# Sharing the PSUM copies of a projected product between two engines, in a triangle-multiplication and spectral kernel

## The chip, the cores and the metric

The kernel runs on one core of one Trainium2 chip. The metric is the device time of the whole program in microseconds, as the median of repeated runs. The core's engines have queues of their own, each worked off in order: PE (TensorE: matmuls and transposes, with PEld for the loading of weights), DVE (VectorE), ACT (ScalarE), POOL (GpSimd) and SP (SyncE, which issues most DMAs here). They meet at semaphores. PE writes into PSUM, and DVE and ACT read from there.

## What is computed

The input x has 512 x 512 positions with 64 channels. Layer 0 normalises it, gates two projections with a mask, multiplies them as a matrix product per channel, normalises that over the channels, projects it, gates it again and adds it to x. Layer 1 takes 12 x 12 Fourier modes of the result, mixes the channels and adds the inverse transform. The part that matters here is the normalisation of the product over the channels and its projection (the two lines that begin with `out = _ln` and `out = out @ out_w`).

```
x = x + _L0_conv_ref(_gn(x), ...)          # layer 0
    xn = _ln(x, norm_w, norm_b)
    left  = (xn @ left_w  + left_b)  * mask * sigmoid(xn @ lgate_w + lgate_b)
    right = (xn @ right_w + right_b) * mask * sigmoid(xn @ rgate_w + rgate_b)
    out_gate = sigmoid(xn @ ogate_w + ogate_b)
    out = einsum('bkjd,bkid->bijd', left, right)
    out = _ln(out, onorm_w, onorm_b)
    out = out @ out_w + out_b
    return out * out_gate
x = x + _L1_conv_ref(_gn(x), ...)          # layer 1: fft2, 12 x 12 modes, channel mixing, ifft2
```

## The kernel before

Rows whose mask is zero add nothing to the product, so the kernel gathers those whose mask is not zero into at most 256 ranks, and works on a product of 256 x 256 positions (`places`, in SBUF). The stages that lead there end at about 659 us of the span. Then one long loop (L1137) does two things in one sequence of steps s: first the *projected stage*, 64 groups that normalise and project the product, and then 256 groups that gate the result, add it to x and gather statistics (the gating loop, to about 1490 us). The last stage, to 1815 us, adds the inverse transform and stores the output.

A group is 8 x 64 = 512 elements per partition, and eight groups make a block (SIZE = 8); in step s = 8 k + n, n counts inside the block. The order of the instructions is the one written down (the schedule is manual). A step takes a group g through these stations, some steps apart:

- `transpose(s + 13)` (L979): PE transposes the group in four matmuls into `t_ps` (two buffers), and ACT copies it into `xt_y` (L988; two buffers).
- `centered(s + 12)` (L998): eight matmuls of 64 x 128 with the weights `both`. They write `y_ps`: in each half, 64 columns of the centred product and 64 of the projected one. It has two buffers, so that product g + 2 may start only when all readers of product g are done.
- `squared(s + 12)` (L1014): ACT squares the centred columns into `sq_c` (L1023) and then copies the projected columns into the group's slot of `xt_c` (L1024), a ring of 15 buffers.
- `summed(s + 11)` (L1026), in every other step: DVE sums the squares of two groups into `scratch`, a tile in PSUM.
- `root(k + 1)` (L1032), at n = 5: ACT takes the square root of a block's sums, once the sum of its last group (g % 8 = 7) is there. The first root loads ACT's table of functions.
- The reciprocal at n = 7 (L1204), on DVE.
- The multiplication `z_t` (L1211), DVE: the projected product, copied 12 steps earlier, times the reciprocal root. POOL adds the bias for two groups at a time (L1215), and SP stores the result in DRAM (`u_d`, L1220).

In the first 12 steps (the lead, LEAD = 13) there is no multiplication yet. POOL also issues the first gathers of x for the gating loop (L637) in this stage. When the last product is done, `y_ps` is closed and its PSUM goes to the matmuls of the gating loop (`c_ps`, `w_ps`; L1148).

Of the kernel before, what the change touches and what calls it, by code (L numbers as in the profile page):

```python
# [19 lines left out]
C = 64  # L20
# [26 lines left out]
def conv_preact_kernel(ctx: ExitStack, tc: tile.TileContext, t: dict):  # L47
    nc = tc.nc
# [572 lines left out]
    def compact(fc):  # L621
# [31 lines left out]
        with tc.tile_pool(name="xc", bufs=1) as cp:  # L653
# [56 lines left out]
            with tc.tile_pool(name="fb", bufs=QB + 8) as gp, tc.tile_pool(name="fw", bufs=2) as wk, tc.tile_pool(  # L710
# [18 lines left out]
                def centered(q):  # L729
                    cps = pc.tile([P, 8, C], F32, name="cc_ps")  # L730
                    for i in range(4):
                        nc.tensor.matmul(
                            cps[:, 2 * i : 2 * i + 2, :], gts[q][:, i * P : (i + 1) * P], center, start=True, stop=True
                        )
                    sq = wk.tile([P, 8, C], F32, name="sqc")
                    nc.scalar.activation(sq, cps, AF.Square)
                    k, n = divmod(q, QB)
                    if n == 0:
                        totals[k] = rp.tile([P, QB * 8], F32, name="total")
                    return sq, totals[k][:, 8 * n : 8 * n + 8]  # L740
# [82 lines left out]
        with tc.tile_pool(name="tri", bufs=1) as trp:  # L823
# [17 lines left out]
            with tc.tile_pool(name="ti", bufs=4) as ip, tc.tile_pool(name="tt", bufs=3) as tp, tc.tile_pool(  # L841
                name="tpt", bufs=4, space=PSUM
            ) as ps_t, tc.tile_pool(name="tpo", bufs=3, space=PSUM) as ps_o:
                for c in range(C):
                    sides = []
                    for name, src in (("left", left_d), ("right", right_d)):
                        raw = ip.tile([P, 2, K], F32, name=name + "_raw")
# [26 lines left out]
            SIZE = 8  # L874
            LEAD = 13
# [5 lines left out]
            with tc.manual_schedule(), tc.tile_pool(name="late", bufs=1) as lp:  # L881
# [65 lines left out]
                with tc.tile_pool(name="np_x", bufs=LEAD + 2) as tp, tc.tile_pool(  # L947
# [63 lines left out]
                    def raw(s):  # L1011
                        return xts[s].rearrange("p i (h c) -> p (i h) c", h=2)

                    def squared(s, cps):  # L1014
                        n = s % SIZE
                        if n % 2 == 0:
                            sqs[s // 2] = sqp.tile([P, 16, C], F32, name="sq_c")
                        sq = sqs[s // 2][:, 8 * (n % 2) : 8 * (n % 2) + 8, :]
                        if s >= first * SIZE:
                            nc.scalar.activation(sq, cps, AF.Square)  # L1020
                        else:
                            by_half = lambda t: t.rearrange("p (i h) c -> p h i c", h=2)
                            nc.scalar.activation(by_half(sq), cps[:, :, :, :C], AF.Square)  # L1023
                            nc.scalar.copy(by_half(raw(s)), cps[:, :, :, C:])  # L1024

                    def summed(s):  # L1026
                        k, n = divmod(s, SIZE)
# [109 lines left out]
                    for s in range(-LEAD, total_g + 2 * SIZE):  # L1137
# [16 lines left out]
                        if 0 <= s + LEAD - 1 < total_g:  # L1154
                            cps = centered(s + LEAD - 1)
# [9 lines left out]
                        if cps is not None:  # L1165
                            squared(s + LEAD - 1, cps)
# [304 lines left out]
```

## Time and profile before

| | |
|---|---|
| Median of three runs | 1818.94 us (1818.11 to 1819.47) |
| The profiled execution | 1816.82 us, its span 1815.0 us |
| Busy in the span | PE 1641.3 (90%), DVE 1424.5 (78%), ACT 961.3 (53%), POOL 945.1 (52%) |
| Projected stage, 659 to 768 us | PE 107.8, DVE 76.2, ACT 101.4, POOL 61.3 us busy of 109.0 |
| Change of stage, 768 to 800 us | PE 30.8, DVE 26.5, ACT 26.6, POOL 25.6 of 32.0 |
| Gating loop, 800 to 1490 us | PE 657.1, DVE 662.5, ACT 500.9, POOL 650.5 of 690.0 |
| Last stage, 1490 to 1815 us | PE 246.6, DVE 181.4, ACT 24.8, POOL 60.7 of 325.0; DMA engines busy throughout, 418 GB/s |
| Copies of the projected product (L1024) | 64 on ACT, 0.58 us each |

The profile is that of one execution, so its own time stands beside its span; the median of the runs is another figure. Shares of busy time over the span mix stages with different limits, and a stage is read by itself. Two instructions of one engine may overlap by about 0.1 us in the records, so that the distance from start to start says more about an engine's pace than the duration of one. The ends of matmuls are modelled, their starts are recorded.

### The profile page before, as it was taken

How to read it: one execution, taken by the hardware profiler on the slowest of the kernel's cores; microseconds unless marked ns; L12 is line 12 of the kernel's file. 1: busy time of each engine (PE TensorE's matmuls, PEld its weight loads, DVE VectorE, ACT ScalarE, POOL GpSimd, SP SyncE). 2: the span in 40 equal slices, each digit the busy share in tenths (PEclk: the TensorE clock that was granted, in tenths of full speed). 3: DMA queues.
4: the chain of work that ended last, by engine and by line, in shares of the span. 5: the costliest groups of instructions: out<-in, count | busy, mean ns of one | idle time of the engine just before them, and what ended most of it. 6: DMA issues, size and time to landing. Idle time of an engine off the chain costs nothing. (4 is left out here: it accounts for less than half of the span.)

```text
span 1815.0 us, 33640 instructions
## 1 busy us (share of the span) xinstructions
PE 1641.3 (90%) x11424; PEld 1287.8 (71%) x11424; DVE 1424.5 (78%) x2980; ACT 961.3 (53%) x1708; POOL 945.1 (52%) x711
## 2 busy tenths in 40 slices
PE   6779899999899999998999999999999977998772
PEld 6667666664688778897888888888888844665331
DVE  7989777777455547779999999999999996765442
ACT  3666555554222259986777777777777741011000
POOL 4665111111000006788999999999999892211120
PEclk9989999999899999999999999999999986555555
DMA  7999155556655513577777776777677689999999
GB/s 286 386 386 380 72 138 137 140 140 153 203 176 184 175 47 133 213 256 254 259 239 242 265 246 234 256 267 260 238 259 271 220 261 418 425 427 426 427 426 385
DMA packets 189525, 467.94 MB, mean 258 GB/s; under 512 B 34848, under 2 KB 134176, under 8 KB 148384
## 3 DMA queue, kind: packets, MB, share of 16 engines
q1 hardware_dynamic: 158160, 262.09, 42.5%
q0 software_dynamic: 27712, 201.40, 29.0%
q10 hardware_dynamic: 3472, 2.20, 0.5%
q8 instruction: 93, 1.52, 0.3%
q14 instruction: 88, 0.72, 0.1%
HBM read 278.05 MB, written 187.56 MB: 257 GB/s over the span
## 5 line engine op out<-in xcount | busy, mean ns | idle before, releaser
L995 PE MATMUL w_ps<-gate_x,xt_c 128*128 128x128 f32 x2048 | 281.1, 281 | 28.9 <-DVE z_t L1211 27.3
L1058 POOL TENSOR_TENSOR places<-places,z_t 128x1024 f32<-128x1024 f32 x127 | 301.0, 2370 | 8.1
L995 PEld LDWEIGHTS w_ps<-gate_x,xt_c 128*128 128x128 f32 x2048 | 252.6, 194 | 45.1 <-DVE z_t L1211 43.6
L995 PE MATMUL c_ps<-center_x,xt_c 128*128 128x128 f32 x2048 | 277.6, 279 | 1.2 <-ACT xt_c L1024 0.6
L995 PEld LDWEIGHTS c_ps<-center_x,xt_c 128*128 128x128 f32 x2048 | 253.6, 195 | 3.9 <-ACT xt_c L990 2.8
L1377 PE MATMUL l_ps<-places,rinv 24*128 24x512 f32 x512 | 207.4, 1127 | 30.1 <-DVE places L1384 18.8
L1113 DVE BATCH_NORM_STATS2 stats2c<-places 128x6 f32<-128x128 f32 x1024 | 220.4, 278 | 8.4 <-POOL places L1058 8.4
L1028 DVE TENSOR_REDUCE scratch<-sq_c 128x16 f32<-128x1024 f32 x160 | 194.5, 1216 | 27.9 <-ACT sq_c L1023 19.4
L1215 POOL TENSOR_TENSOR z_t<-z_t,bias_row_out 128x1024 f32<-128x1024 f32 x32 | 75.6, 2364 | 247.8 <-DVE z_t L1211 243.7
L1162 ACT ACTIVATE z_t<-z_t 128x1024 f32<-128x1024 f32 x128 | 135.5, 1058 | 130.6 <-DVE z_t L1217 129.1
L985 PE MATMUL t_ps<-c_ident,places 128*128 128x128 f32 x1280 | 199.6, 279 | 1.3 <-DVE places L870 1.3
L1377 PEld LDWEIGHTS l_ps<-places,rinv 24*128 24x128 f32 x512 | 120.3, 304 | 112.3 <-DVE places L1384 57.0
L985 PEld LDWEIGHTS t_ps<-c_ident,places 128*128 128x128 f32 x1280 | 145.1, 142 | 60.6 <-issue 52.9
L990 ACT ACTIVATE xt_c<-t_ps,ab_xc 128x512 f32<-128x512 f32 x256 | 176.0, 687 | 13.2 <-PE t_ps L985 12.1
L1211 DVE TENSOR_TENSOR z_t<-w_ps,rs_n 128x512 f32<-128x512 f32 x256 | 171.9, 672 | 8.3 <-PE w_ps L995 8.2
L1020 ACT ACTIVATE sq_c<-c_ps 128x512 f32<-128x512 f32 x256 | 150.5, 588 | 32.5 <-PE c_ps L995 32.0
L1217 DVE TENSOR_TENSOR z_t<-z_t,scratch 128x1024 f32<-128x1024 f32 x128 | 156.3, 1221 | 9.9 <-ACT rs_n L1034 3.7
L687 DVE BATCH_NORM_STATS2 stats1c<-x_ps 128x6 f32<-128x512 f32 x256 | 156.6, 682 | 8.0 <-PE x_ps L686 7.6
L1054 POOL TENSOR_TENSOR z_t<-z_t,places 128x1024 f32<-128x1024 f32 x64 | 151.5, 2368 | 13.9 <-ACT z_t L1162 13.8
L1384 DVE TENSOR_TENSOR places<-places,l_ps 128x512 f32<-128x512 f32 x176 | 109.2, 682 | 55.8 <-DMA places<-x_h,dst_i 43.9
L1054 POOL TENSOR_TENSOR z_t<-z_t,bias_row_out 128x1024 f32<-128x1024 f32 x63 | 149.3, 2370 | 5.7 <-ACT z_t L1162 5.4
L749 POOL COPY rbc<-rq_out 128x512 f32<-128x512 f32 x64 | 38.3, 613 | 210.2 <-DVE rq_out L214 132.0
(213 smaller groups left out, 2746.9 us busy)
## 6 DMA issues: line engine op xcount, KB each, us to landing
x_h<-places SPq DMA_DIRECT2D x64, 1024.0 KB
out_x<-places SPq DMA_DIRECT2D x44, 1024.0 KB
places<-u_d SPq DMA_DIRECT2D x512, 64.0 KB
out_x<-lx_t SPq DMA_DIRECT2D x20, 1024.0 KB
left_d<-o_c SPq DMA_DIRECT2D x64, 256.0 KB
right_d<-o_c SPq DMA_DIRECT2D x64, 256.0 KB
left_raw<-left_d SPq DMA_DIRECT2D x64, 256.0 KB
right_raw<-right_d SPq DMA_DIRECT2D x64, 256.0 KB
```

Of the source, the lines that this page charges most:

```text
L687: nc.vector.bn_stats(stats[:, 0, 16 * (jc % quarter) + 4 * r + c, :], ps.rearrange("p i k -> p (i k)"))
L985: nc.tensor.transpose(tps[:, i, :], flat[:, o : o + P], ident)
L990: nc.scalar.activation(xts[s], tps, AF.Identity, bias=ab1[:, 2:3])
L995: nc.tensor.matmul(ps[:, 2 * i : 2 * i + 2, :], xts[s][:, i, :], w, start=True, stop=True)
L1020: nc.scalar.activation(sq, cps, AF.Square)
L1028: nc.vector.tensor_reduce(totals[k % 2][:, 8 * (n - 1) : 8 * (n + 1)], sqs.pop(s // 2), AX.X, ALU.add)
L1054: nc.gpsimd.tensor_mul(zs[k, c], zs[k, c], u)
L1058: nc.gpsimd.tensor_add(xr, xr, zs.pop((k, c)))
L1113: nc.vector.bn_stats(st[k // 4][:, g, k % 4, :], x_of(k)[:, :, 2 * g : 2 * g + 2])
L1211: nc.vector.tensor_mul(z[:, 8 * odd : 8 * odd + 8, :], wps, rs)
L1217: nc.vector.tensor_add(z, z, bias_ps["ogate"].unsqueeze(1).to_broadcast([P, 16, C]))
L1377: nc.tensor.matmul(ps.rearrange("p j o -> p (j o)"), rinv[h, b, :], it[h], start=True, stop=True, tile_position=(32 * g, 0),)
```

## The change

Of the copies of the projected product (L1024), DVE makes some in place of ACT: those of the odd groups, except the last of each block (g % 8 = 7) once the lead is over (g from 13 on). These are 3 of 8 in the later blocks, and 1, 3, 5, 7, 9 and 11 in the lead; 25 of 64 in all. The place in the order of the step is the same; on DVE it is ahead of that step's sum, reciprocal and multiplication. In the steps of odd groups there is no sum. No other line changes; line numbers behind it rise by one.

```diff
@@ squared(s, cps) @@
                         else:
                             by_half = lambda t: t.rearrange("p (i h) c -> p h i c", h=2)
                             nc.scalar.activation(by_half(sq), cps[:, :, :, :C], AF.Square)
-                            nc.scalar.copy(by_half(raw(s)), cps[:, :, :, C:])
+                            mine = s % 2 == 1 and (s < LEAD or s % SIZE != 7)
+                            (nc.vector.tensor_copy if mine else nc.scalar.copy)(by_half(raw(s)), cps[:, :, :, C:])
```

Here `s` is the group, which the loop passes as `s + LEAD - 1`.

## The prediction

> **What bounds the kernel now.** I read the busy time by stretches first, to find the stage that the change touches. The projected stage runs from 660 to 769 us; this is its steady middle, four blocks of eight groups (stretch, its length, then busy us and instruction counts of PE, weight load, DVE, ACT and POOL, the granted clock, the DMA share, GB/s):
>
> ```profile
> 691.23:744.94 53.71, 53.71 (x642) 44.45 (x641) 43.15 (x52) 50.53 (x101) 37.78 (x16) 1.00 0.39 157
> ```
>
> 53.71 us for 32 groups is 1.678 us per group. PE is busy all of it at a full clock, ACT 94%, DVE 80%. ACT and PE are close, so the timeline must tell which one leads. One group of it (start, duration, engine, line, operation, and in brackets the idle time before it):
>
> ```profile
> 665.06 0.60 ACT L1023 ACTIVATE sq_c<-y_ps 128x512 f32<-128x512 f32 x1
> 665.53 0.97 PEld L1006 LDWEIGHTS y_ps<-both,xt_y 64*128 64x128 f32 x16 [0.17 <-issue]
> 665.53 1.16 PE L1006 MATMUL y_ps<-both,xt_y 64*128 64x128 f32 x16
> 665.56 0.58 ACT L1024 COPY xt_c<-y_ps 128x512 f32<-128x512 f32 x1
> 666.02 0.60 ACT L988 COPY xt_y<-t_ps 128x512 f32<-128x512 f32 x1
> 666.62 0.65 PE L985 MATMUL t_ps<-c_ident,places 128*128 128x128 f32 x4
> 666.74 0.60 ACT L1023 ACTIVATE sq_c<-y_ps 128x512 f32<-128x512 f32 x1
> ```
>
> The product y_ps starts at 665.53 and ends at 666.69; the square that reads it starts at 666.74. ACT was free from about 666.5 (its instructions follow each other at 0.46 to 0.50 us when nothing is awaited), so ACT waits for PE. PE itself goes from y_ps to t_ps (1.09 us) and back to the next y_ps (0.59 us, with the gap of 0.17 us called issue): 1.68 us, the whole period. The copy into xt_y that the next product needs ends at 666.62, 0.59 us before that product starts at 667.21. So PE leads, and ACT has room. The one place where that turns round is the loading of the square root's table:
>
> ```profile
> 676.71 1.28 ACT L1034 ACT_TABLE_LOAD   x1
> 678.01 0.31 ACT L1034 ACTIVATE rs_n<-scratch,eps 128x64 f32<-128x64 f32 x1
> 678.22 0.59 ACT L1023 ACTIVATE sq_c<-y_ps 128x512 f32<-128x512 f32 x1
> 678.70 0.59 ACT L1024 COPY xt_c<-y_ps 128x512 f32<-128x512 f32 x1
> 679.16 0.61 ACT L988 COPY xt_y<-t_ps 128x512 f32<-128x512 f32 x1
> 679.82 1.16 PE L1006 MATMUL y_ps<-both,xt_y 64*128 64x128 f32 x16 [0.80 <-ACT xt_y L988]
> ```
>
> Here PE waits 0.80 us for xt_y, behind table load, root, square and copy. Behind it ACT catches up at 1.43 us per group (squares at 678.22, 679.64, 681.07). In the whole stage PE waits for ACT here and at its start (0.4 us), before any copy. DVE in the steady part (718.07 is n = 5 of a block, 721.50 n = 7):
>
> ```profile
> 718.07 0.69 DVE L1211 TENSOR_TENSOR z_t<-xt_c,scratch 128x512 f32<-128x512 f32 x1 [0.85 <-ACT rs_n L1034]
> 718.86 1.23 DVE L1028 TENSOR_REDUCE scratch<-sq_c 128x16 f32<-128x1024 f32 x1
> 720.18 0.69 DVE L1211 TENSOR_TENSOR z_t<-xt_c,scratch 128x512 f32<-128x512 f32 x1
> 720.90 0.56 DVE L1204 RECIPROCAL scratch<-rs_n 128x64 f32<-128x64 f32 x1
> 721.50 0.69 DVE L1211 TENSOR_TENSOR z_t<-xt_c,scratch 128x512 f32<-128x512 f32 x1
> 723.60 1.28 DVE L1211 TENSOR_TENSOR z_t<-xt_c,scratch 128x512 f32<-128x512 f32 x2
> ```
>
> From start to start: multiplication to sum 0.79, sum to multiplication 1.32, multiplication to multiplication 1.28 - 0.69 = 0.59, to the reciprocal 0.72, from it 0.60. Two groups need 0.79 + 1.32 + 0.59 = 2.70 us, the two with the reciprocal 3.43; a block 3 x 2.70 + 3.43 = 11.5 of 8 x 1.678 = 13.4 us. 1.9 us per block are free.
>
> **ACT loses 25 copies.** Of 32 odd groups the seven with g % 8 = 7 from 15 on stay. That frees 25 x 0.46 = 11.5 us of ACT's queue. It lies beside PE's 1.68 us per group, so I cost it at nothing, except at the table load: group 9, whose copy stands between square and xt_y there, is an odd one. What is worth there depends on when DVE's copy of it ends, because product 11 also needs that buffer of y_ps.
>
> **DVE gains 25 copies.** The trace has no DVE copy of this shape. The nearest row is another DVE copy of 128x512 f32 out of PSUM, the farthest one of the same size whose output is scattered element by element:
>
> ```profile
> L857 DVE COPY left_t<-side_ps 128x512 f32<-128x512 f32 x64 | 42.9, 675 | 4.1 <-PE side_ps L852 4.1
> L1359 DVE COPY places<-it_ps 128x512 f32<-128x512 f32 x2 | 2.1, 1028 | 0.8 <-PE it_ps L1356 0.8
> ```
>
> Bounds: ACT's 0.58 below, 1.03 above. Here the output lies in runs of 64 elements, for which ACT pays nothing (0.58 against 0.60 us flat), so I take 0.675.
>
> **What the copy waits for.** The built program lets DVE's copy wait for ACT, not PE: it stands behind the square of the same group, which reads the other columns of the same tile. The trace shows such an order already: the multiplication above waits 0.85 us for a root whose result it does not use; both read the tile scratch. So copy 9 starts at 678.22 + 0.59 + 0.04 = 678.85 and ends at 679.53; xt_y 11 now starts at 678.70 and ends at 679.31. Product 11 starts at 679.53 + 0.04 = 679.57 instead of 679.82: **0.25 us gained**. The Trainium skill, "PSUM — Partial Sum Buffer", section "PSUM bank collisions raise a hardware error", says that two engines may not touch one bank in the same partitions at once, reads included, and so speaks against a copy that runs beside its square. Without the rule copy 9 would be done before the table is loaded, product 11 would start at 679.31 + 0.05, and the gain would be 0.46 us.
>
> **Does DVE keep up?** A copy between two multiplications adds 0.58 (0.675 less the 0.10 us by which neighbours overlap) to 0.68 us. A block with three: 11.5 + 1.7 to 2.0 = 13.2 to 13.5 of 13.4 us. DVE is then full. The waits of 0.85 and about 0.4 and 0.75 us that are its idle time vanish. Within a block the two groups with the reciprocal need 3.43 + 0.6 = 4.0 us against 3.36, so the next copy is 0.65 us late, and the two groups without a copy (2.70 against 3.36) make it good. A copy may be late by this: on time it ends 0.65 + 0.04 + 0.675 = 1.37 us after its product's end, and product g + 2 starts 2.20 us after it (666.69 to 668.89): 0.83 us. 0.65 is less, so PE does not wait: 0.
>
> **What is queued behind the copies on DVE.** The multiplications of older groups, and the sums. The sum of group 8k + 7 gates the root: before, it started 0.70 us after its product's end; now it follows copy, multiplication, sum and two multiplications (4.07 us) of a copy that is 0.65 us late, and starts about 2.0 us after it, 1.3 later. It had 1.2 us of room (sum over at 756.74, root at 757.97). So ACT may wait some 0.1 us per block, and gets 0.46 us back two instructions later, before PE needs anything from it. POOL's additions come up to 1.3 us later, but it idles 30% here. Behind them in its queue are the first gathers of x (754.41; landing within 7.5 us), read from 766.48 on: 4 us spare. The store of u_d follows the additions on SP. At the stage's end DVE enters up to 1 us late, and its waits of 0.71 and 1.16 us (768.93, 772.09) swallow that. Copy 63, for which PE waits at 769.42, stays on ACT.
>
> **PE's extra wait.** 25 products now wait for DVE and ACT. Where the trace has PE waiting for two, an extra instruction stands before it:
>
> ```profile
> L763 PEldq EVENT_SEMAPHORE  x126: 51/51/51, 221.6 to 455.3; - x126
> ```
>
> The first of these ran at 221.57, 0.5 us ahead of the weight load that it guards (222.07), while PE still worked off the rows before, the last of which began at 221.86. So 0; if exposed, 25 x 0.051 = 1.3 us lost.
>
> **Sum.** The profiled execution took 1816.82 us (span 1815.0 and 1.8 around it). 1816.82 - 0.25 = 1816.57. The median of the runs is 1818.94, 2.12 above; so **1818.7 us**. The stages behind it keep their order and start 0.25 us earlier; the end is a chain of DMAs that follows them.
>
> **Rivals.** (A) The forecast, 1818.7: 60%. (B) PE's extra waits are exposed: 1818.7 + 1.3 = 1820.0. For it: PE leads, each of its ns counts. Against: the row at 221.57. 14%. (C) Slower, **DVE becomes the bound**: at 1.03 us a copy adds 0.93 to 1.03, a block needs at least 11.5 + 2.8 = 14.3 us against 13.4; PE then waits for y_ps. 51 groups behind the lead are 6.4 blocks: 6.4 x 0.9 = 5.7, less the 0.83 us that a copy may be late, 4.9, and the time 1823.8. It decides from a copy of about 0.75 us on (11.5 + 3 x 0.65 = 13.4). Against: L857. 14%, of which half below 1822. (D) Faster, **ACT leads and PE's full row is only how its ends are modelled**: 25 x 0.46 = 11.5 us, 1807.4. For it: ACT at 94%, and t_ps starting at the very end of xt_y (666.62). Against: 1.43 us per group when ACT has to catch up, and the 0.59 us between xt_y and its product. 12%.
>
> **How the numbers follow.** A measurement of this kernel can tell about 0.2% (3.6 us) from no change. A, B and 0.05 of C lie within it: 0.79; D 0.12; the rest of C 0.09. The range 1816.6 to 1822.0 holds A with the bounds of its terms (0.8 us gained at most at the table load, 1.3 lost), the spread of the runs (1818.11 to 1819.47) and the lower half of C; it leaves out D and the upper half of C, 0.2.
>
> **What would show it.** In the profile after: 39 copies at L1025 on ACT and 25 on DVE of 0.65 to 0.70 us; DVE at about 95% of the steady stretch (43.15 + 12 x 0.65 of 53.7) and ACT at about 84% (50.53 - 12 x 0.46), the stretch still 53.7 us; PE's wait at the table load at about 0.55 us; the wait of DVE for the root gone. Wrong if PE waits for DVE's copy in the stage, if 16 products take other than 16 x 1.68 us, or if a copy takes over 0.75 us.

## The result and the profile after

The changed kernel is slower: 1823.39 us (median of 10 runs, 1820.51 to 1826.27) against 1819.57 us (1817.56 to 1822.55) of the kernel before, run beside it. The ratio is 1.0022, with a 95% interval of 1.0012 to 1.0031: by the ratio 4.0 us lost (2.2 to 5.6), where 0.25 us of gain was forecast.

The same steady stretch of the projected stage in the profile after (columns as before: stretch, length, busy us and instructions of PE, weight load, DVE, ACT and POOL, granted clock, DMA share, GB/s):

```profile
691.23:744.94 53.71, 52.65 (x628) 43.48 (x628) 48.04 (x63) 44.37 (x87) 35.90 (x16) 1.00 0.39 154
```

PE is no longer busy all of it: 1.06 us of idle time, in a stretch that was full before. ACT fell from 50.5 to 44.4 us, DVE rose from 43.2 to 48.0 only, since less work fitted into the stretch. DVE is not full either, with 5.7 us free. So no engine is busy all the time, which may mean a chain of waits that goes round over several of them.

The copies, in the view of their line:

```profile
L1025 ACT COPY xt_c<-y_ps x39: 580/580/611, 663.5 to 772.4; 128x512 f32<-128x512 f32 x39
L1025 DVE COPY xt_c<-y_ps x25: 683/691/692, 665.3 to 769.9; 128x512 f32<-128x512 f32 x25
...
  ACT sq_c L1023: 18.9, 13
...
  PE y_ps L1006: 2.1, 6
```

A DVE copy takes 0.691 us, near the 0.675 of the forecast. The third line is the idle time ahead of these copies (us, times): 18.9 us, 13 times, waiting for ACT's square; the lead's waits are in it. The last says that PE waited six times for a copy; one of these is group 11's wait at the table load (0.7 us), the other five are new waits of the later blocks. Who waited for whom in the whole stage:

```profile
ACT rs_n L1035 <- DVE z_t L1212: 3.6, 5, 0.8
PEld y_ps L1006 <- ACT xt_y L988: 2.8, 6, 0.9
...
PE y_ps L1006 <- DVE xt_c L1025: 2.1, 6, 0.7
```

ACT's root waits for DVE's multiplication, DVE's copies for ACT's square, and PE for both engines. The first two close a ring, which the timeline around one root shows (start, duration, engine, line, operation, idle time before it and what ended it):

```profile
731.98 1.23 DVE L1029 TENSOR_REDUCE scratch<-sq_c 128x16 f32<-128x1024 f32 x1
733.30 0.69 DVE L1212 TENSOR_TENSOR z_t<-xt_c,scratch 128x512 f32<-128x512 f32 x1
734.02 0.31 ACT L1035 ACTIVATE rs_n<-scratch,eps 128x64 f32<-128x64 f32 x1 [0.75 <-DVE z_t L1212]
734.24 0.59 ACT L1023 ACTIVATE sq_c<-y_ps 128x512 f32<-128x512 f32 x1
734.71 0.59 ACT L988 COPY xt_y<-t_ps 128x512 f32<-128x512 f32 x1
734.86 0.69 DVE L1025 COPY xt_c<-y_ps 128x512 f32<-128x512 f32 x1 [0.87 <-ACT sq_c L1023]
735.66 1.00 PEld L1006 LDWEIGHTS y_ps<-both,xt_y 64*128 64x128 f32 x16 [0.32 <-ACT xt_y L988]
```

At 731.98 DVE sums group 8k + 7. The root needs this sum, but it does not start when the sum ends (733.21). It starts when the multiplication behind the sum has ended (733.99): both read the tile scratch, and the program keeps their order. ACT idles 0.75 us for that. Behind the root stands the square of group 1 of the next block; DVE's copy of that group waits for the square, and DVE idles 0.87 us. So DVE, which is late, waits for ACT, which waits for DVE. Once round it: 0.84 us from root to copy, 11.08 us of DVE's instructions from that copy to the start of the next sum of a group 8k + 7, 1.32 to the multiplication behind it and 0.72 to the root, 13.96 us together; from root to root the trace has 13.96 to 13.98 us in each of the stage's last six distances. PE needs 13.42 for a block.

What PE loses of it shows at two products in each block; the first (group 43 at 735.66) is the last line above, the other is group 47, which waits for the copy of group 45:

```profile
741.93 0.68 DVE L1025 COPY xt_c<-y_ps 128x512 f32<-128x512 f32 x1
742.73 1.00 PEld L1006 LDWEIGHTS y_ps<-both,xt_y 64*128 64x128 f32 x16 [0.49 <-ACT sq_c L1023]
742.76 1.16 PE L1006 MATMUL y_ps<-both,xt_y 64*128 64x128 f32 x16 [0.28 <-DVE xt_c L1025]
```

From the starts of the products: 0.19 us over 1.68 at group 43, 0.35 at 47, and the same in each block from group 32 on. The first of these waits is group 31's (0.33); up to there the queues swallow the lateness. From the first product to the 64th the stage takes 108.92 us, where it took 106.57: 2.35 us lost. More is lost behind it. From product 0 to the product of group 76, where the gating loop finds its pace, it is 130.49 against 127.02 us, 3.47 in all. Of the difference of 1.1 us about half lies where PE waits for gathers of x, the second wait below above all:

```profile
782.77 0.63 PE L985 MATMUL t_ps<-c_ident,places 128*128 128x128 f32 x4 [0.28 <-DMA places<-in_x,src_i]
789.57 0.63 PE L985 MATMUL t_ps<-c_ident,places 128*128 128x128 f32 x4 [1.05 <-DMA places<-in_x,src_i]
```

These waits are not in the trace of before. The other half needs no gather: DVE's multiplications themselves are late. The last ten of them start 0.55 us later behind product 63 than before; in the kernel root_early of the experiments they are late by the same 0.55 us, no transpose waits for a gather, and group 76 is late by just 0.55 us.

The rest of the 7.2 us between the two profiled executions (1816.82 and 1824.04) lies outside this stretch: 1.3 us ahead of the projected stage, before any changed instruction, and 2.5 us behind group 76. Single executions differ by more there: over all the profiles here the stage starts between 656.9 and 663.1 us, and the stretch from group 76 to the end takes 1025.6 to 1031.5 us, 1031.5 also in the kernel lead, which loses nothing in the stage. Whether the change costs anything in these places, these profiles can't show.

### The profile page after: what moved, and what is told of

The parts are those of the page before. It is cut to its first block, busy times and chain, and to the rows that moved or that the text cites. A ratio compares the mean times of both kernels' runs of the same rounds, so it can differ in the third digit from the quotient of the medians.

```text
span 1822.3 us, 33641 instructions
## 1 busy us (share of the span) xinstructions
PE 1643.9 (90%) x11424; PEld 1286.8 (71%) x11424; DVE 1438.5 (79%) x3005; ACT 952.1 (52%) x1683; POOL 945.4 (52%) x711
## 4 chain that ended last, share of the span: by engine, by line
PE 48%; DVE 25%; DMA 11%; issue 5%; ACT 4%; POOL 4%; SPq 1%; POOLq 0%; another core or an unknown queue 0%; DVEq 0%; ACTq 0%
PE tri_c_ps L866 7%; PE w_ps L995 6%; PE c_ps L995 6%; PE l_ps L1378 5%; DVE z_t L1212 5%; DVE scratch L1029 5%; DMA places<-x_h,dst_i 4%; DVE stats2c L1114 4%; DVE stats1c L687 3%; PE t_ps L985 3%; PE sides_c L763 3%; DVE z_t L1218 3%; DMA lx_t<-x_h,dst_i 3%; PE cc_ps L732 3%; PE gates_c L763 3%
## 5 line engine op out<-in xcount | busy, mean ns | idle before, releaser
L1114 DVE BATCH_NORM_STATS2 stats2c<-places 128x6 f32<-128x128 f32 x1024 | 220.4, 278 | 13.1 <-POOL places L1059 13.1
```

Source lines behind the costliest of these rows:

```text
L1114: nc.vector.bn_stats(st[k // 4][:, g, k % 4, :], x_of(k)[:, :, 2 * g : 2 * g + 2])
```

## The experiments

The times of one kernel's runs spread by 4 to 8 us (0.2 to 0.5%), and a comparison resolves about 0.1%. The distances inside the stage repeat to some hundredths of a us, so the theories are told apart by these. "Root to root" is the usual distance of two roots in the later blocks, "stage" goes from the start of product 0 to that of product 63, "to 76" from product 0 to that of group 76; all are read from the starts in the trace. The ratio is to the kernel before on the same chip.

| kernel | DVE copies | root to root | stage | to 76 | ratio, 95% interval |
|---|---|---|---|---|---|
| before | 0 | 13.42 | 106.57 | 127.02 | |
| before_again | 0 | | 106.57 | 127.03 | 0.9991 (0.9980 to 1.0001) |
| lead | 6 | 13.42 | 106.42 | 126.88 | 1.0004 (0.9995 to 1.0013) |
| two13 | 18 | 13.44 | 106.43 | 126.88 | 1.0011 (1.0002 to 1.0019) |
| two35 | 19 | 13.66 | 107.50 | 128.41 | 1.0011 (1.0003 to 1.0020) |
| after | 25 | 13.97 | 108.92 | 130.49 | 1.0022 (1.0012 to 1.0031) |
| again | 25 | 13.97 | 108.94 | 130.38 | 1.0022 (1.0013 to 1.0031) |
| root_behind | 25 | 13.42 | 106.31 | 127.11 | 1.0008 (1.0000 to 1.0017) |
| root_early | 25 | 13.68 | 107.87 | 128.87 | 1.0018 (1.0007 to 1.0029) |
| no_last | 22 | 13.97 | 108.74 | 129.19 | 1.0023 (1.0012 to 1.0034) |
| all_odd | 32 | 14.50 | 112.24 | 133.78 | 1.0047 (1.0033 to 1.0061) |
| preload | 0 | 13.42 | 105.70 | 126.16 | 0.9996 (0.9987 to 1.0006) |

**again**: the changed kernel, unaltered.

> The changed kernel once more. Stage means from the start of the first product y_ps to the start of the 64th: 106.57 us before, 108.92 after; from the first product to that of group 76, behind the change of stages: 127.02 before, 130.49 after. If what was lost lies in the order of the engines' queues and not in the spread of the runs, both numbers come back within 0.3 us (108.9 and 130.5), and the time is 3 to 5 us above that of before.

108.94 and 130.38 us came back, and 1.0022 for the time. The loss inside the stage and at its end belongs to the program, not to one execution.

**root_behind**: the order of two instructions on ACT, and nothing else.

```diff
-                        if n == 5 and 0 <= k + 1 < first + len(units):
+                        behind = s + LEAD - 1 < first * SIZE
+                        if n == 5 and 0 <= k + 1 < first + len(units) and not behind:
                             root(k + 1)
                         if cps is not None:
                             squared(s + LEAD - 1, cps)
+                        if n == 5 and 0 <= k + 1 < first + len(units) and behind:
+                            root(k + 1)
```

> The changed kernel with the root of a block behind the square of the same step on ACT, while products last. Theory (a loop over two engines): root, square of group 1, three copies with their sums and multiplications on DVE, sum of group 7, multiplication, root again take 13.96 us per block against PE's 13.42; DVE's 0.87 us of idle time ahead of the first copy lies in that loop. With the root behind the square the copy finds its square done, the 0.87 us go, the loop needs about 13.1 us, PE leads again: stage 106.4 us (2.5 less than after), products all 1.68 us apart, time within 0.1% of before. Rival 1 (DVE has too much work, or its copies run slow beside ACT's reads): nothing changes, 108.9. Rival 2 (PE pays for its 25 double waits): 108.9.

The steady stretch and the same place of the timeline in this kernel:

```profile
690.00:743.71 53.71, 53.71 (x644) 44.46 (x644) 50.37 (x65) 45.88 (x89) 37.81 (x16) 1.00 0.40 158
```

```profile
714.18 1.23 DVE L1029 TENSOR_REDUCE scratch<-sq_c 128x16 f32<-128x1024 f32 x1
715.50 0.69 DVE L1215 TENSOR_TENSOR z_t<-xt_c,scratch 128x512 f32<-128x512 f32 x1
715.78 0.60 ACT L1023 ACTIVATE sq_c<-y_ps 128x512 f32<-128x512 f32 x1
716.28 0.31 ACT L1035 ACTIVATE rs_n<-scratch,eps 128x64 f32<-128x64 f32 x1
716.41 0.69 DVE L1025 COPY xt_c<-y_ps 128x512 f32<-128x512 f32 x1 [0.23 <-ACT sq_c L1023]
```

PE is full again. The square now stands ahead of the root and starts as soon as its product is there; the root that follows waits for nothing. The copy's 0.23 us of idle time is DVE being early. All 25 copies are still on DVE, and PE still has the 25 extra instructions with which a product waits for two engines (the double waits):

```profile
L1006 PEldq EVENT_SEMAPHORE  x25: 51/51/51, 662.9 to 764.6; - x25
```

DVE is even busier than in the changed kernel (50.4 us against 48.0 in a stretch of the same length). The stage takes 106.31 us, as expected, and every product but group 11's comes 1.68 us behind the one before. So neither the amount of work, nor the copies' speed, nor the double waits made the loss. The ring did, and it is broken at ACT's order. The whole time is 1.0008 of before (1.0000 to 1.0017).

**two13**: two copies per block in place of three. Groups 1 and 3:

```diff
-                            mine = s % 2 == 1 and (s < LEAD or s % SIZE != 7)
+                            mine = s % 2 == 1 and (s < LEAD or s % SIZE in (1, 3))
```

> Two of eight behind the lead (groups 1 and 3 of a block) in place of three; the lead as in the changed kernel. Loop: one copy less takes 0.6 us out of it, 13.96 - 0.61 = 13.35 is under 13.42, so nothing is lost: stage 106.4 us, time within 0.1% of before. Rival 1, work in proportion (19 copies of 25): about 108.2; rival 2, 19 double waits of 25: about 108.3.

106.43 us: nothing is lost in the stage. (It has 18 copies, not the 19 that the expectation counts.) Without the copy of group 5 the ring is almost as short as PE's block: 13.44 us from root to root, not the 13.35 expected and 0.02 over PE's 13.42. The sum of group 8k + 7 comes later by these 0.02 us in each block (1.30 us behind its product's end at group 23, 1.39 at 63), and the stage ends before a product is late. The whole time is nevertheless 1.0011 of before (1.0002 to 1.0019). Since the kernel before against itself came out at 0.9991, a tenth of a per cent is not a finding here; in this execution the first 52 groups behind group 76 took 146.4 us where before took 144.5 and 144.2. That is a place where executions of one program differ (see before_again).

**two35**: the same count at other places, groups 3 and 5.

```diff
-                            mine = s % 2 == 1 and (s < LEAD or s % SIZE != 7)
+                            mine = s % 2 == 1 and (s < LEAD or s % SIZE in (3, 5))
```

> Two of eight behind the lead, groups 3 and 5 in place of 1 and 3; same count as two13. Loop: group 1's copy stays on ACT, so DVE's multiplication at n = 5 waits for the root itself, and the two copies stand later in the loop, nearer to the sum that the root waits for: a block needs about 13.6 us, stage 107.0 (0.5 over two13). A theory by the count of copies or by DVE's work gives the same as two13, 106.4.

107.50 us and 13.66 from root to root, against 106.43 and 13.44. The place of the copies counts (two35 has one copy more, that of group 13), which no theory by their number or by DVE's work gives: one copy in one block does not lengthen every block. The stage lost more than expected (1.1 over two13, not 0.5).

**all_odd**: all four odd groups of a block.

```diff
-                            mine = s % 2 == 1 and (s < LEAD or s % SIZE != 7)
+                            mine = s % 2 == 1
```

> All odd groups, 32 copies. Loop: one copy more makes a block 13.96 + 0.61 = 14.57 us, 1.15 over PE's; in seven blocks less what the queues can swallow the stage takes about 112.6 us (6 more than before), the time is 7 to 8 us above before. Rival 1, DVE's work alone (11.5 + 4 x 0.6 = 13.9 of 13.42): at most 0.5 per block, under 110. Rival 2, 32 double waits: 109.5.

The waits in its stage:

```profile
ACT rs_n L1035 <- DVE z_t L1212: 7.2, 6, 1.3
...
PE y_ps L1006 <- DVE xt_c L1025: 5.6, 12, 0.7
```

112.24 us and 14.50 from root to root: the fourth copy adds 0.53 us per block, close to its whole slot on DVE of 0.60, as work inside the ring does; DVE's work alone, 13.9 us in the expectation, falls short of 14.50. The root's waits double in sum (3.6 us in the changed kernel). The time is 1.0047 of before, 8.5 us.

**lead**: the six copies of the lead alone.

```diff
-                            mine = s % 2 == 1 and (s < LEAD or s % SIZE != 7)
+                            mine = s % 2 == 1 and s < LEAD
```

> The six copies of the lead alone on DVE. Loop: there are no multiplications yet, nothing is lost, and the copy that stands behind the table load is off ACT's path: PE's wait for group 11 shrinks from 0.87 to 0.72 us, stage 106.4 us, time within 0.1% of before. Rivals that charge each copy (its double wait, or a slow read beside ACT): 6 of 25 of 2.35 us, stage 107.1.

106.42 us, 0.15 less than before. This is the one gain that the change has, at the table load.

**root_early**: the root written behind the sum of group 7, ahead of the multiplication of that step.

```diff
-                        if n == 5 and 0 <= k + 1 < first + len(units):
+                        if n == 5 and 0 <= k + 1 < first + len(units) and s + LEAD - 1 >= first * SIZE:
                             root(k + 1)
...
                             summed(s + LEAD - 2)
+                        if n == 4 and s + LEAD < first * SIZE and k + 1 >= 0:
+                            root(k + 1)
```

> The changed kernel, with the root of a block written right behind the sum of group 7, ahead of the multiplication of that step, while products last. In the changed kernel the root waits for that multiplication too (both read the tile scratch), 0.7 us. Here it waits for the sum alone, but ACT's next copy into xt_y stands between root and square of group 1, and DVE's multiplication now waits for the root. By the loop a block needs 13.75 us (13.96 in the changed kernel, 13.1 with the root behind the square, 13.42 for PE alone): stage 108.1 us, 0.8 less than the changed kernel, 1.7 more than root_behind. If the multiplication is not in the loop, the stage is at 108.9 or above.

107.87 us and 13.68 from root to root: less than the changed kernel, more than root_behind, as expected to 0.3 us. The multiplication behind the sum is a member of the ring. (Of the 1.3 us over before, 0.2 is lost at the table load, which now stands ahead of group 10's copy into xt_y.)

**no_last**: the copies of the last block back on ACT.

```diff
-                            mine = s % 2 == 1 and (s < LEAD or s % SIZE != 7)
+                            mine = s % 2 == 1 and (s < LEAD or s % SIZE != 7) and s < 56
```

> The changed kernel, with the copies of the last block (groups 57, 59 and 61) back on ACT. The question is the 1.1 us that the changed kernel loses behind its last product, between group 64 and group 76, most of it where PE's transposes wait for gathers of x that POOL issued late. If DVE's lateness at the end of the projected stage makes them late, a last block of 11.5 us lets DVE catch up and the loss goes: stage 108.6 us (group 63 no longer waits for a copy), product 0 to group 76 129.0 (130.4 in the changed kernel). If the late gathers are the spread of the runs or have another cause, the second number is 130.0.

108.74 us, and 129.19 us to group 76: from product 63 to group 76 it takes 20.45 us as before (20.45), where the changed kernel takes 21.57. No transpose waits for a gather there any more. So the second part of the loss, 1.1 us, comes from DVE's lateness at the end of the stage. How it gets into the gathers is shown in part only. Counted from product 63, the gather behind the longer wait was issued at 8.36 us before and at 8.92 in again, 0.56 us later through POOL's queue; it landed at 14.70 and at 18.61, so its transfer took 9.7 us in place of 6.3. Why it took longer no run shows. The whole time does not show the 1.3 us (1.0023, an interval of 0.2%).

**preload**: the kernel before, with one extra square root of a 128 x 1 tile ahead of the loop.

```diff
                     nc.vector.memset(eps, EPS)
+                    warm = lp.tile([P, 1], F32, name="warm")
+                    nc.scalar.activation(warm, eps, AF.Sqrt)
```

> The kernel before, with one square root of a 128 x 1 tile on ACT ahead of the loop, which loads the table of functions while ACT waits for the first transposes; no copy is moved. The load of 1.28 us then lies in ACT's idle time ahead of group 0, PE's 0.87 us of wait before group 11 go: stage 105.7 us, and if the stages behind just follow, the time is 0.9 us (0.05%) under before. If ACT was not what PE waits for there, stage 106.6.

```profile
657.82 1.28 ACT L974 ACT_TABLE_LOAD   x1 [1.80 <-issue]
659.11 0.20 ACT L974 ACTIVATE warm<-eps 128x1 f32<-128x1 f32 x1
659.75 1.07 ACT L990 COPY xt_y<-t_ps 128x512 f32<-128x512 f32 x2 [0.43 <-PE t_ps L987]
```

The table is loaded while ACT waits for the first transposes, which it still awaits afterwards (0.43 us). The stage takes 105.70 us, 0.87 less than before: all that PE lost at the table load, almost six times what six copies on DVE got back. In the whole time 0.05% can't be told from none (0.9996, 0.9987 to 1.0006).

**before_again**: the kernel before, as a measure of the comparison.

> The kernel before, once more, as a measure of what the comparison can tell. Stage 106.6 us, product 0 to group 76 127.0, ratio 1.000 within its interval. Open is whether its first gated halves of the gating loop (third and following) start 34 us after group 76 in every run, or in some 37 to 38 us as in two of the variants: if both are seen here, the 1 to 2 us that root_behind and two13 lie above before are the spread of that place.

The stage is the same to 0.01 us. The ratio of 0.9991 shows what is left of the spread over 11 and 35 runs. The question about the gated halves is answered in part by other traces. The place is POOL's second multiplication with the product read back from u_d: it starts 34.1 us behind group 76 in both profiles of this kernel, but 37.8 us in the changed kernel, where POOL waits 3.7 us for that DMA, and 34.2 in again, which is the same program. So this place differs from execution to execution. The later start (37.1 to 37.8 us) is in four of the eight profiles with DVE copies in the later blocks (after, root_behind, two13, root_early) and in none of the four without; whether such copies make it more likely stays open.

## Why the prediction was wrong

- **What bounds the stage**: right. PE leads before, and with the ring broken it leads again with 25 copies on DVE.
- **ACT's 25 copies are worth nothing but at the table load**: right. The gain there was put at 0.25 us; the wait of group 11's product fell from 0.87 to 0.72 us over the usual distance, so 0.15.
- **The price of a DVE copy**: right, 0.691 us against 0.675 taken, a slot of 0.60 us between multiplications. That it waits for its square was right too.
- **"The waits of 0.85 and about 0.4 and 0.75 us that are its idle time vanish"**: this is the step that failed. DVE's instructions of a block come to 13.1 us (13.96 less 0.87), a little under the 13.2 to 13.5 computed and under PE's 13.42. But the wait of 0.85 us for the root did not vanish; it came back as 0.87 us ahead of the copy of group 1, whose square stands behind the root on ACT. I had added up DVE's work and compared it with PE's, as if DVE could start on it at any time.
- **"So ACT may wait some 0.1 us per block, and gets 0.46 us back two instructions later"**: the same error from ACT's side. The root waits 0.75 us, not 0.1. The sum was late about as forecast: it starts 1.8 us behind its product's end at group 23 and 2.0 from group 31 on, where it took 0.7 before. The room was wrong: I counted 1.2 us from the end of the sum, but the root waits for the multiplication behind the sum too. In the profile before:

```profile
756.83 0.69 DVE L1211 TENSOR_TENSOR z_t<-xt_c,scratch 128x512 f32<-128x512 f32 x1
757.97 0.34 ACT L1034 ACTIVATE rs_n<-scratch,eps 128x64 f32<-128x64 f32 x1
```

  The multiplication ends at 757.52, so the room was 0.45 us; 1.1 to 1.3 us of lateness less 0.45 leaves 0.65 to 0.85, near the 0.6 to 0.8 that the roots wait. The view of L1211 before even has such a wait once, among those who waited for it:

```profile
  ACT rs_n L1034: 0.9, 1
```

  And I judged the root's lateness by whether PE gets its xt_y in time, not by whether DVE, whose lateness it is, gets its square. A wait that is harmless once is added in every block when it lies in a ring.
- **"0.65 is less, so PE does not wait"**: it holds up to group 30. From then on the lateness has grown past the room of 0.83 us that the prediction gave it, and group 8k + 7 waits 0.35 us for the copy two groups before it.
- **"4 us spare" for the gathers**: worked out for the first gather, with 12 us to its use. The later one that PE waits for had 2.4 us before (landed 14.70 us behind product 63, read at 17.12), and its transfer took 3.4 us longer in again than before, which I had not counted on.
- **"At the stage's end DVE enters up to 1 us late"**, which two of its waits were to swallow: they do so in part. 0.55 us of DVE's lateness reaches group 76, and with the gathers it is 1.1 us.
- **PE's double waits cost nothing**: right; in root_behind products with and without them are 1.68 us apart.
- **The rivals**: the time lies past the range, near rival C (DVE becomes the bound), but not by its mechanism. C needed a copy of over 0.75 us. The loss came at 0.69 us, through a wait that C counted as free too. D fell with the trace, where PE waits and nothing is gained, and B with root_behind.

The sum by the terms as measured is 2.35 in the stage (0.15 of gain at the table load included) and 1.1 behind it, near 3.5 us; the ratio gives 4.0 (2.2 to 5.6).

## What to carry to other kernels

Work moved to an engine with free time fits only if that free time is not itself a wait inside a ring: follow each wait of the receiving engine back, and if it returns to that engine within one turn of the loop, the turn's length is its work plus those waits, to be set against the leader's pace. When no engine is full and yet each waits for another, look for such a ring before moving work, and try the order of two instructions first; here one exchange on ACT gave back all that the stage had lost. Lateness that does no harm once must be asked whether it comes back in the next turn.

## What the runs showed of the hardware beyond this

The distances between products inside this stage repeat within 0.1 us, and the stage itself within 0.02 us, from execution to execution (106.57 twice, 108.92 and 108.94), while whole runs of one kernel spread by 4 to 8 us. The stages around it, in which engines wait for DMAs, carry much of that spread: the start of the first product lay between 656.9 and 663.1 us in kernels that are the same up to there, but for one small square root, and the stretch from group 76 to the end took 1025.6 to 1031.5. A loss of 2.4 us is smaller than that spread of runs, and plain in two traces.
